# Dummy matmuls of a GAT and gated-GNN kernel: a float32 product with 64 columns in place of a bfloat16 product with 256

## The chip, the cores and the metric

The kernel runs on one core of one Trainium2 chip. The metric is the device time of one execution in microseconds (us). A core has five engines that run side by side: TensorE (PE in the profile, with its weight loads as PEld), VectorE (DVE), ScalarE (ACT), GpSimd (POOL) and SyncE (SP), which issues most of the transfers.

## The reference

A batch of 32 graphs with 512 nodes and 128 features goes through two layers that share one adjacency matrix. Cut to what is computed:

```python
# layer 0: graph attention, with a residual
h = relu(layernorm(x)) @ W                       # (32, 512, 128)
logits = leaky_relu(h @ a_src [:, :, None] + h @ a_dst [:, None, :], 0.2)
alpha = softmax(logits + where(adj > 0, 0, -1e9))
x = x + leaky_relu(alpha @ h + b, 0.3)
# layer 1: five steps of a gated recurrence, with a residual
h = relu(layernorm(x))
for _ in range(5):
    m = adj @ h                                  # used for in and out matrix alike
    z = sigmoid([m, m] @ w3.T + b3 + h @ u3.T + bu3)
    r = sigmoid([m, m] @ w4.T + b4 + h @ u3.T + bu3)
    hv = tanh([m, m] @ w5.T + b5 + (r * h) @ u5.T + bu5)
    h = (1 - z) * h + z * hv
x = x + h
```

## The kernel before, in words

Each of the 32 graphs is one tile of work: 512 nodes as four blocks of 128. Layer 0 of a graph normalizes `x` on VectorE and ScalarE, transposes it (`t_a`, L707, for the first four graphs; by transfers for the others), multiplies by the attention weights (`hp`, L812), spreads the source scores over the partitions (`es`, L847, again for the first four), weighs the adjacency (`pt`, L897) and averages (`av`, L928). Each of the five steps of layer 1 multiplies by the adjacency in two float16 halves (`m`, L1037), makes the gates (`g`, L1056, L1057 and L1077) and the candidate (`v`, L1100 and L1101), and updates the state `hT` on VectorE. The last graph has an ending of its own, with `v_end` (L1288) and `end` (L1276 and L1306).

Ahead of the graphs, TensorE turns the weight matrix (`gwT_ps`, L456), multiplies it by the attention vectors (`wa_ps`, L463: a float32 product with two columns), and turns the adjacency (`at_ps`, L494) once its 1 MB has arrived in `a_sb`.

The order of the instructions on each engine is not found while the kernel runs. Every piece of work is a `Task` with an engine, an estimated length, a key and the tasks that it needs. `plan` simulates the engines with the constants in `COST` and gives the tasks back in the order of their simulated begins; they are issued in that order, and `pin` keeps it. An engine then works through its list strictly in that order and waits at an instruction whose inputs are not there.

The change touches one kind of task, the dummy matmul. There are `FIRST_IDLE` = 32 and `IDLE` = 36 of them, 68 in all. Nothing needs them and nothing reads what they write, which is one tile of PSUM, the bank `f_idle`. Their key is 1e12, so the planner takes one for TensorE where no other task can begin, the first 32 from 500 ns of its own time on and the rest from 6500 ns on. Their estimated lengths are these:

```python
    for i in range(FIRST_IDLE + IDLE):
        add("PE", [480 if i < FIRST_IDLE else 256], 1e12, idle, (), (f_idle,),
            at=500 if i < FIRST_IDLE else 6500)
```

Both operands are views of a constant 1.0 that the start of the program writes with GpSimd.

Of the kernel before, what the change touches and what calls it, by code (L numbers as in the profile page):

```python
# [10 lines left out]
F32 = mybir.dt.float32  # L11
# [4 lines left out]
P = 128  # L16
# [272 lines left out]
def gat_then_gated_gnn_kernel(  # L289
# [20 lines left out]
    nc = tc.nc  # L310
# [23 lines left out]
    def new(buffer, name, shape=(P, N), dtype=F32):  # L334
        tag = buffer.tags[0]
        if "bank" in buffer.tags:
            buffer.tile = psum.tile([P, N], F32, tag="bank", name=name)
        elif tag in ("way", "turn", "line"):
            buffer.tile = dram.tile(list(shape), F32, tag=tag, name=name)
        else:  # L340
            buffer.tile = pools[BUFFERS[tag]].tile(list(shape), dtype, tag=tag, name=name)
        return buffer.tile
# [94 lines left out]


    f_idle = Buffer("v", "bank")
    unit = nc.const_aps.tensor(1.0, [P, 2 * P], mybir.dt.bfloat16)  # L440

    def idle():
        pin(nc.tensor.matmul(  # L443
            (f_idle.tile or new(f_idle, "idle"))[:, : 2 * P], lhsT=unit[:, :P], rhs=unit,
            start=True, stop=True,
        ))

# [3 lines that stand above are left out]
# [946 lines left out]
```

## Time and profile before

| | before |
|---|---|
| median of 3 runs | 1136.21 us (1136.18 to 1140.1) |
| profiled execution, its own time | 1136.34 us |
| profiled execution, its span | 1134.6 us |
| PE busy | 1127.7 us, 99% of the span |
| DVE busy | 875.4 us, 77% |
| ACT busy | 661.5 us, 58% |
| POOL busy | 351.5 us, 31% |
| dummy matmuls (L443) | 68 instructions, 11.5 us busy |

The span runs from the first to the last instruction; the execution's own time has 1.7 us more. A busy PE is not a PE at its peak: matmuls are pipelined, and the profile gives each a modelled end, so that their records overlap. How long a matmul occupies the engine is therefore read from the distance of one start to the next, not from its duration. One product in the program can be several records: a float32 product shows as two matmuls and two weight loads, a bfloat16 or float16 product as one of each.

### The profile page before, as it was taken

The page shows a single profiled execution, that of the slowest core. Times are in us where ns is not written, and L with a number is a line of the kernel's source. Part 1 is how long each engine was busy: PE and PEld are TensorE (multiplying, and loading weights), DVE is VectorE, ACT ScalarE, POOL GpSimd, SP SyncE. Part 2 cuts the span into 40 slices and gives each one's busy share as a digit, 9 for nine tenths or more (in the row PEclk, how much of TensorE's full clock was granted, in tenths as well). Part 3 has the DMA queues.
Part 4 walks back from the last instruction along what each step waited for, and adds up shares of the span by engine and source line. Part 5 has one row for each costly group of instructions (what it writes and reads, how often), then busy time and mean ns, then how long its engine had stood idle before and what let it go on. Part 6 is the DMA issues. An engine that isn't in the chain of part 4 may idle for free.

```text
span 1134.6 us, 14335 instructions
## 1 busy us (share of the span) xinstructions
PE 1127.7 (99%) x4334; PEld 592.6 (52%) x4334; DVE 875.4 (77%) x2002; ACT 661.5 (58%) x1299; POOL 351.5 (31%) x504
## 2 busy tenths in 40 slices
PE   9999999999999999999999999999999999999998
PEld 8655555455455545555544555555555554444444
DVE  7888968887687788879777777889888976745655
ACT  6756656645655565656566556665656564555553
POOL 4255432511431344244134214453544230100000
PEclk9999999999999999999999999999999999999999
DMA  3245453643444554355345345454655343331321
GB/s 108 57 88 112 84 108 84 126 88 84 105 81 102 85 121 93 86 120 106 89 102 107 73 100 103 111 101 114 117 116 103 75 76 84 47 74 29 84 74 67
DMA packets 188498, 104.52 MB, mean 92 GB/s; under 512 B 152192, under 2 KB 167680, under 8 KB 188288
## 3 DMA queue, kind: packets, MB, share of 16 engines
q1 hardware_dynamic: 170512, 66.57, 25.4%
q0 software_dynamic: 17472, 36.79, 17.6%
q8 instruction: 36, 0.59, 0.2%
q14 instruction: 46, 0.38, 0.1%
q10 hardware_dynamic: 432, 0.20, 0.1%
HBM read 39.46 MB, written 30.47 MB: 62 GB/s over the span
## 4 chain that ended last, share of the span: by engine, by line
PE 99%; DMA 0%; DVE 0%; SPq 0%; issue 0%; DVEq 0%
PE m L1037 24%; PE g L1077 12%; PE g L1057 12%; PE g L1056 12%; PE v L1101 12%; PE v L1100 12%; PE av L928 10%; PE hp L812 3%; DMA a_sb<-in_adj_dram 0%; PE idle L443 0%; PE at_ps L494 0%; PE t_b L707 0%; PE t_a L707 0%; PE es L847 0%; PE v_end L1288 0%; PE end L1306 0%
## 5 line engine op out<-in xcount | busy, mean ns | idle before, releaser
L1062 ACT ACTIVATE rs<-g,zrb 128x512 f32<-128x512 f32 x160 | 109.6, 685 | 122.7 <-PE g L1057 121.9
L1114 DVE SCALAR_TENSOR_TENSOR d<-hv,hT 128x512 f32<-128x512 f32 x158 | 108.2, 685 | 92.9 <-ACT hv L1107 91.9
L1107 ACT ACTIVATE hv<-v,vb 128x512 f32<-128x512 f32 x159 | 108.8, 684 | 106.6 <-PE v L1101 106.3
L1069 DVE SCALAR_TENSOR_TENSOR rh<-rs,hT 128x512 f32<-128x512 f32 x160 | 109.5, 685 | 71.2 <-ACT rs L1062 70.5
L1056 PE MATMUL g<-hT,u3T 128*128 128x512 f32 x320 | 163.4, 592 | 0.0
L1057 PE MATMUL g<-mT,w4sT 128*128 128x512 f32 x320 | 163.4, 592 | 0.0
L1077 PE MATMUL g<-mT,w3dT 128*128 128x512 f32 x320 | 162.8, 593 | 0.0
L1101 PE MATMUL v<-rh,u5hT 128*128 128x512 f32 x318 | 162.4, 592 | 0.0
L1100 PE MATMUL v<-mT,w5sT 128*128 128x512 f32 x318 | 162.4, 592 | 0.0
L1037 PE MATMUL m<-adjT,hi 128*128 128x512 f16 x640 | 161.9, 379 | 0.0
L1037 PE MATMUL m<-adjT,lo 128*128 128x512 f16 x640 | 160.7, 379 | 0.0
L650 POOL TENSOR_TENSOR rs_b<-ve_b,mhalf 128x4 f32<-128x4 f32 x32 | 36.9, 1154 | 384.2 <-DVE ve_b L630 161.4
L1089 ACT ACTIVATE zs<-g,zrb 128x512 f32<-128x512 f32 x160 | 109.4, 685 | 68.0 <-PE g L1077 66.7
L1048 ACT COPY mT<-m 128x512 f32<-128x512 f32 x160 | 92.9, 583 | 81.7 <-PE m L1037 79.1
L928 PEld LDWEIGHTS av<-hw,pt 128*128 128x128 f32 x1024 | 123.5, 191 | 21.1 <-issue 17.5
L928 PE MATMUL av<-hw,pt 128*128 128x129 f32 x1024 | 125.0, 275 | 0.1
L1123 DVE SCALAR_TENSOR_TENSOR hT<-d,hT 128x512 f32<-128x512 f32 x158 | 109.3, 692 | 11.9
L1237 ACT CAST hiT<-hT 128x512 f16<-128x512 f32 x128 | 78.9, 616 | 66.2 <-DVE hT L1123 64.2
L1037 PEld LDWEIGHTS <-hi 128*128 128x128 f16 x640 | 62.6, 98 | 98.6 <-issue 45.0
L1120 DVE SCALAR_TENSOR_TENSOR d<-zs,d 128x512 f32<-128x512 f32 x158 | 109.2, 691 | 5.2
L1037 PEld LDWEIGHTS <-lo 128*128 128x128 f16 x640 | 62.6, 98 | 90.5 <-issue 25.3
L1240 DVE TENSOR_TENSOR loT<-hT,hiT 128x512 f16<-128x512 f32 x128 | 87.6, 687 | 17.7 <-ACT hiT L1237 16.3
(141 smaller groups left out, 1351.7 us busy)
## 6 DMA issues: line engine op xcount, KB each, us to landing
x<-in_x_dram SPq DMA_DIRECT2D x32, 256.0 KB, 2.9
out_dram<-res SPq DMA_DIRECT2D x31, 256.0 KB, 2.3
turn_a<-blocks_a POOLq DMA_DIRECT2D x112, 64.0 KB, 2.7
h0T<-turn_a POOLq DMA_DIRECT2D x28, 256.0 KB, 4.0
es<-line POOLq DMA_DIRECT2D x28, 256.0 KB, 4.3
turn_b<-blocks_b POOLq DMA_DIRECT2D x112, 64.0 KB, 2.6
hT<-turn_b POOLq DMA_DIRECT2D x28, 256.0 KB, 3.9
way<-blocks SPq DMA_DIRECT2D x28, 256.0 KB, 2.3
```

Source lines behind the costliest of these rows:

```text
L928: pin(nc.tensor.matmul(avs()[:, i, :], lhsT=f_pts[c].tile[:, ts(2 * part + i, P)], rhs=hw()[:, c, : D + 1], start=start, stop=(c == K - 1) ...
L1037: pin(nc.tensor.matmul(f_m.tile, lhsT=part[:, k, :], rhs=adjT[:, k, :], start=(first and k == 0), stop=(not first and k == K - 1),))
L1056: pin(nc.tensor.matmul(g, lhsT=u3T, rhs=hT, start=True, stop=False))
L1057: pin(nc.tensor.matmul(g, lhsT=w4sT, rhs=f_mT.tile, start=False, stop=True))
L1062: pin(nc.scalar.activation(new(f_r, f"rs_{b}_{step}"), f_g.tile, AF.Tanh, bias=rb, scale=0.5))
L1069: pin(nc.vector.scalar_tensor_tensor(new(f_rh, f"rh_{b}_{step}"), f_r.tile, 1.0, hT, ALU.add, ALU.mult))
L1077: pin(nc.tensor.matmul(f_g.tile, lhsT=w3dT, rhs=f_mT.tile, start=False, stop=True, skip_group_check=True))
L1089: pin(nc.scalar.activation(new(f_z, f"zs_{b}_{step}"), f_g.tile, AF.Tanh, bias=zb, scale=0.5))
L1100: pin(nc.tensor.matmul(v, lhsT=w5sT, rhs=f_mT.tile, start=True, stop=False))
L1101: pin(nc.tensor.matmul(v, lhsT=u5hT, rhs=f_rh.tile, start=False, stop=True))
L1120: pin(nc.vector.scalar_tensor_tensor(d, f_z.tile, 1.0, d, ALU.add, ALU.mult))
L1123: pin(nc.vector.scalar_tensor_tensor(hT, f_d.tile, 0.5, hT, ALU.mult, ALU.add))
```

## The change

The constant becomes a float32 matrix of 128 x 128 in place of a bfloat16 one of 128 x 256. The dummy product takes the whole of it as the stationary operand and its first 64 columns as the moving one, and writes 64 columns of the PSUM tile in place of 256. The number of dummy tasks, their keys and their estimated lengths stay, so the planner's order stays too.

```diff
     f_idle = Buffer("v", "bank")
-    unit = nc.const_aps.tensor(1.0, [P, 2 * P], mybir.dt.bfloat16)
+    unit = nc.const_aps.tensor(1.0, [P, P], F32)
 
     def idle():
         pin(nc.tensor.matmul(
-            (f_idle.tile or new(f_idle, "idle"))[:, : 2 * P], lhsT=unit[:, :P], rhs=unit,
+            (f_idle.tile or new(f_idle, "idle"))[:, : P // 2], lhsT=unit, rhs=unit[:, : P // 2],
             start=True, stop=True,
         ))
```

## The prediction

> **What bounds the kernel now.** I read the page's busy times and its chain first, to learn whether PE time is worth anything, then PE's waits, then PE's timeline around the dummy matmuls. The page:
>
> ```profile
> PE 1127.7 (99%) x4334; PEld 592.6 (52%) x4334; DVE 875.4 (77%) x2002; ACT 661.5 (58%) x1299; POOL 351.5 (31%) x504
> PE 99%; DMA 0%; DVE 0%; SPq 0%; issue 0%; DVEq 0%
> ```
>
> The chain that ended last is PE for 99% of the span. All that PE ever waited for is in its list of waits over the whole run:
>
> ```profile
> PE at_ps L494 <- DMA a_sb<-in_adj_dram: 1.1, 1, 1.1
> PE idle L443 <- PEq L1384: 0.8, 1, 0.8
> PE end L1306 <- DVE gated L1299: 0.2, 1, 0.2
> ```
>
> Two lie in the first 8 us and one at the end. In the 1100 us between, PE goes from one product to the next, so a nanosecond added to PE there moves the end by a nanosecond, whatever the other engines do. This list can miss waits of up to 0.16 us, because a record's modelled end lies that far beyond the 0.11 us after which the next may start; so I look for cover in the distances of starts. The dummies are at these places of PE's timeline up to 8 us:
>
> ```profile
> 0.78 3.45 PE L443 MATMUL idle<-const-bfloat16-1.0 128*128 128x256 bf16 x17 [0.78 <-PEq L1384]
> 4.07 0.27 PE L456 MATMUL gwT_ps<-ident,gw 128*128 128x128 f32 x1
> 4.18 0.61 PE L443 MATMUL idle<-const-bfloat16-1.0 128*128 128x256 bf16 x4
> 4.70 0.38 PE L463 MATMUL wa_ps<-acols,gwT 128*128 128x2 f32 x2
> 4.94 1.16 PE L443 MATMUL idle<-const-bfloat16-1.0 128*128 128x256 bf16 x9
> ```
>
> The reader is to see 30 dummies in a prologue that ends with the wait for the adjacency, at 7.22 us. The other 38 stand in groups of one to seven: 28 from 8.7 to 31 us, then one at 106, 978 and 990 us and seven at 1014.5 us. Of these two windows are typical:
>
> ```profile
> 17.82 0.94 PE L443 MATMUL idle<-const-bfloat16-1.0 128*128 128x256 bf16 x7
> 18.60 0.28 PE L812 MATMUL hp<-wrow,h0T 128*128 128x131 f32 x1
> ...
> 1014.45 0.94 PE L443 MATMUL idle<-const-bfloat16-1.0 128*128 128x256 bf16 x7
> 1015.23 1.03 PE L1037 MATMUL m<-adjT,hi 128*128 128x512 f16 x4
> ```
>
> Seven dummies take 0.78 us from their first start to that of the next product in both: 0.111 us each, and the next product follows without a gap. The dummies fill what the planner took for a gap; in the trace the gap is not longer than they are.
>
> In the first block the starts lie about 0.215 us apart up to 3.72 us (0.94, 1.16, 1.37 and so on), and 0.11 us from there. PE ran at half pace for 2.94 us after its first matmul, although the page shows the granted clock as full.
>
> [...]
> - [...] `v` at L1100 with 512 columns starts at 31.06 and the next product at 31.93, 0.87 us, against 0.217 us for a float16 product with 512 columns (four of `m` in 0.87 us): a factor of 4.0. So 4 x 64 columns stream as long as 1 x 256.
> - [...] 190 ns for a float32 load (`viol_ps`), 99 ns for a bfloat16 one (`idle`).
> [...]
>
> **The change part by part.** It removes 68 bfloat16 products, one load and one matmul each, and adds 68 float32 products, two of each. The order, the bank, the other engines' lists and all transfers stay, and no wait is added: nothing waits for a dummy. The float32 constant is no new work either, since GpSimd writes const-float32-1.0 in the program's start already, at 0.29 us. What remains is one question: **how long does PE need for a float32 product with 64 columns?** The trace has none. Its bounds:
> - Below: the streaming alone, 4 x 64 columns at the pace of the 512-column product, 0.87 / 8 = 0.109 us. That equals the old 0.111; a gain is excluded, because the columns have to stream.
> - Above: two loads that both show, 2 x 0.11 = 0.22 us. Dense `av` records, one load each, start every 0.111 us with a float32 load in each, so a load can't take longer than that in a stream.
> - Nearest row: float32 products with two columns, where nothing streams. For `viol_ps` (PE and PEld in turn):
>
> ```profile
> 938.30 0.28 PE L588 MATMUL viol_ps<-viol,ones 128*128 128x2 f32 x2
> 938.44 1.02 PE L1037 MATMUL m<-adjT,hi 128*128 128x512 f16 x4
> ...
> 938.09 0.41 PEld L588 LDWEIGHTS viol_ps<-viol,ones 128*128 128x128 f32 x2
> 938.33 0.64 PEld L1037 LDWEIGHTS <-hi 128*128 128x128 f16 x4
> ```
>
> Its two matmuls start at 938.30 and 938.33, the next load at 938.33, and the next product at 938.44: 0.14 us for the pair, 0.03 from pass to pass and 0.11 for the load of the product behind. `wa_ps` shows the same: its second load at 4.80, the next load at 4.83, the next product at 4.94. With 64 columns the first pass streams 0.109 / 2 = 0.054 us in place of 0.03, and the second, also 0.054, lies beneath the 0.11 of the next load. I take 0.054 + 0.11 = **0.163 us**, 0.052 more than before, and at half pace double, 0.326 against 0.215.
>
> Prologue (30 dummies), with the same moment of full pace, 3.72 us: 2.94 / 0.326 = 9 dummies go by until then, the other 8 take 1.30, so `gwT_ps` starts at 5.02 in place of 4.07: +0.95. From there to `wa_ps` the four dummies take 0.11 + 4 x 0.163 = 0.76 against 0.62 (where PE waited for ScalarE's copy `gwT`): +0.14. Nine more: +0.47. Together 1.56 us. The cover is the wait for the adjacency: the last dummy starts at about 5.83, `at_ps` could start at 5.94 and starts at 7.22, so 1.28 us are hidden; without that transfer all 1.56 would show. **+0.28** is left. Behind the later `wa_ps` stand ScalarE's four small copies to `wrow` (5.12 to 5.5, then about 6.5), which `hp` needs at 8.95: hidden by 2 us. VectorE's normalization of the first graph needs no PE.
>
> The other 38: 38 x 0.052 = **+1.98**. Cover: two dummies start at 11.42 and 11.53, and `av` could start at 11.64 but starts at 11.86, 0.22 us; `g` at 29.77 is 0.06 late. What these wait for comes from PE itself a little before and moves along, so I count about half, **-0.15**. Everywhere else the next product starts at once, and nothing hides the addition. After 31 us the whole train is late by the same amount.
>
> Sum: 0.28 + 1.98 - 0.15 = +2.1 us. The profiled execution's own time is 1136.34, which becomes 1138.4; it lies 0.13 above the median of 1136.21, so I predict **1138.3** for the median. The 0.163 has both ends: at 0.109, nothing changes (1136.2). At 0.22 (0.43 at half pace) the prologue gains 1.89 + 0.37 + 0.98 - 1.28 = 1.96, the others 38 x 0.11 - 0.15 = 4.03, +6.0 together: 1142.2.
>
> **The rivals.**
> - *The loads hide* (no change, 1136.2). For it: in a dense stream of `av` each float32 load lies beneath 129 columns at no visible cost. Against: beneath 64 columns there is half the time, and `viol_ps` shows 0.11 for the load behind it.
> - *Both loads show* (1142.2). For it: `wa_ps` has its two loads 0.11 apart, and 190 ns records. Against: the 0.03 from pass to pass.
> - *PE stays at half pace* (slower). [...] a float32 dummy streams only 0.109 of 0.163 us, two thirds of its time. If that isn't enough, the 30 dummies go at 0.326 us, `at_ps` starts at about 0.78 + 30 x 0.326 + 0.2 = 10.8 in place of 7.22 (+3.5), real products then run at half pace for up to another 2.94 us (+1.5), and the other 38 add 2.0: +7.0, **1143.2**. It decides if the pace has not changed when the 30 dummies are through. [...]
> - *The change doesn't do what it says*: the planner's lengths would have to move the order, but they are constants; I give it nothing.
>
> **How the numbers follow.** The forecast gets 0.62, the hidden loads 0.18, both loads 0.12, half pace 0.06, a cost above my bounds 0.02. A difference of 0.5%, 5.7 us, is about what a measurement of this kernel can tell from no change (one of three runs lay 0.35% off). The forecast and the hidden loads fall within it, but for 0.02 of the latter below; both loads lie on its edge, half each; half pace is 0.05 outside. That makes 0.02 faster, 0.85 the same, 0.13 slower. The range takes in the hidden loads with a little scatter, 1135.8, and reaches to both loads, 1142.5.
>
> **What would show it right or wrong.** Right: 136 matmul records at L443, pairs 0.16 us apart, seven of them in 1.14 us at 17.8 us; full pace at about 3.7 us; the wait for the adjacency down to zero, `at_ps` at 7.5; from 32 us on all products 1.6 us later, the end 2.1 later. Wrong: pairs at 0.11 or 0.22 us, a half pace that goes on to `at_ps`, or new waits of PE after 32 us.

## The result and the profile after

The changed kernel is slower: 1148.12 us median of 6 runs (1147.47 to 1148.78), against 1140.01 for the kernel before (1136.18 to 1141.07) measured beside it. The ratio is 1.0088, with a 95% interval of 1.0073 to 1.0103. The profiled executions have 1147.68 and 1136.34 us, spans of 1145.9 and 1134.6, so 11.3 us more. The medians lie closer together because the times of the kernel before stand in groups, near 1136.3 and from 1138 to 1141, and four of the six here are late ones. In the larger samples beside the experiments its median is 1136.62 us (35 runs) and 1137.75 (38), so that the 8.1 us between the medians here understate the loss. The last experiment looks at where the groups come from.

The page of the changed kernel, its busy times and its chain:

```profile
PE 1140.2 (100%) x4402; PEld 608.2 (53%) x4402; DVE 876.2 (76%) x2002; ACT 662.2 (58%) x1299; POOL 351.4 (31%) x504
PE 99%; DVE 0%; issue 0%; DVEq 0%
```

PE has 68 records more, 12.5 us more busy time, and still is the chain. All its waits over the run:

```profile
PE idle L443 <- PEq L1384: 0.8, 1, 0.8
PE end L1306 <- DVE gated L1299: 0.2, 1, 0.2
```

The wait for the adjacency, 1.1 us before, is gone: the 1 MB is there, and PE comes to it late. PE's timeline (start, length, line, tile, count) up to the turning of the adjacency and a little beyond:

```profile
0.78 7.49 PE L443 MATMUL idle<-const-float32-1.0 128*128 128x64 f32 x34 [0.78 <-PEq L1384]
8.06 0.42 PE L456 MATMUL gwT_ps<-ident,gw 128*128 128x128 f32 x1
8.27 1.81 PE L443 MATMUL idle<-const-float32-1.0 128*128 128x64 f32 x8
9.87 0.53 PE L463 MATMUL wa_ps<-acols,gwT 128*128 128x2 f32 x2
10.27 4.08 PE L443 MATMUL idle<-const-float32-1.0 128*128 128x64 f32 x18
14.14 1.06 PE L494 MATMUL at_ps<-ident,a_sb 128*128 128x128 f32 x4
14.99 1.06 PE L707 MATMUL t_a<-ident,h 128*128 128x128 f32 x4
15.85 1.01 PE L494 MATMUL at_ps<-ident,a_sb 128*128 128x128 f32 x4
16.69 0.56 PE L443 MATMUL idle<-const-float32-1.0 128*128 128x64 f32 x4
17.09 1.11 PE L812 MATMUL hp<-wrow,h0T 128*128 128x131 f32 x8
```

The first 34 records take 7.28 us up to `gwT_ps`, 0.214 each and **0.43 us a dummy**, and the pace does not change: PE runs at half pace up to 14.14 us. The real products from there still take 0.21 us each (four of `t_a` from 14.99 to 15.85); only at about 16.6 us are they through at 0.11 and less. Two later windows show a dummy at full pace:

```profile
26.45 1.67 PE L443 MATMUL idle<-const-float32-1.0 128*128 128x64 f32 x14
27.96 0.67 PE L812 MATMUL hp<-wrow,h0T 128*128 128x131 f32 x4
...
1025.07 1.67 PE L443 MATMUL idle<-const-float32-1.0 128*128 128x64 f32 x14
1026.58 1.89 PE L1037 MATMUL m<-adjT,hi 128*128 128x512 f16 x8
```

Fourteen records, seven dummies, take 1.51 us from their first start to that of the next product: **0.216 us a dummy** in both, against 0.111 before and 0.163 in the forecast. Within the series the starts lie 0.112 us apart (the second record starts at 26.51, the fourteenth at 27.85). Only the first step is shorter, 0.056.

The starts of the same products in the two profiles give the account. The lines of the kernel before on which its second row rests:

```profile
8.72 0.38 PE L443 MATMUL idle<-const-bfloat16-1.0 128*128 128x256 bf16 x2
8.95 1.13 PE L812 MATMUL hp<-wrow,h0T 128*128 128x131 f32 x8
```

| product | before | after | late by |
|---|---|---|---|
| first `at_ps` | 7.22 | 14.14 | 6.92 |
| first `hp` | 8.95 | 17.09 | 8.14 |
| `hp` behind seven dummies | 18.60 | 27.96 | 9.36 |
| first `v` (L1100) | 31.06 | 41.51 | 10.45 |
| `m` behind the last seven | 1015.23 | 1026.58 | 11.35 |

So 6.9 us are lost in the prologue. Between `at_ps` and `hp` 1.2 are lost, of which the two dummies there make 0.17 (0.40 against 0.23) and the real products at half pace the other 1.05. The 36 dummies behind add 3.2. At 0.105 us more for each, all 38 would add 4.0 where 3.4 show; about 0.6 fell into gaps that were there. One such gap is the 0.22 us ahead of `av`: from the first of the two dummies to `av` it is 0.44 us before (11.42 to 11.86) and 0.43 after (19.61 to 20.04).

### The profile page after: what moved, and what is told of

It reads as the page before. It is cut to its first block, busy times and chain, and to the rows that moved or that the text cites. A ratio compares the mean times of both kernels' runs of the same rounds, so it can differ in the third digit from the quotient of the medians.

```text
span 1145.9 us, 14471 instructions
## 1 busy us (share of the span) xinstructions
PE 1140.2 (100%) x4402; PEld 608.2 (53%) x4402; DVE 876.2 (76%) x2002; ACT 662.2 (58%) x1299; POOL 351.4 (31%) x504
## 4 chain that ended last, share of the span: by engine, by line
PE 99%; DVE 0%; issue 0%; DVEq 0%
PE m L1037 24%; PE g L1077 12%; PE g L1056 12%; PE g L1057 12%; PE v L1100 12%; PE v L1101 12%; PE av L928 10%; PE hp L812 3%; PE idle L443 2%; PE at_ps L494 0%; PE t_a L707 0%; PE es L847 0%; PE t_b L707 0%; PE v_end L1288 0%; PE end L1306 0%; PE end L1276 0%
## 5 line engine op out<-in xcount | busy, mean ns | idle before, releaser
L1100 PE MATMUL v<-mT,w5sT 128*128 128x512 f32 x318 | 162.4, 592 | 0.0
L1057 PEld LDWEIGHTS g<-mT,w4sT 128*128 128x128 f32 x320 | 60.8, 190 | 76.5 <-issue 69.8
```

What stands on the lines that cost most here:

```text
L1057: pin(nc.tensor.matmul(g, lhsT=w4sT, rhs=f_mT.tile, start=False, stop=True))
L1100: pin(nc.tensor.matmul(v, lhsT=w5sT, rhs=f_mT.tile, start=True, stop=False))
```

## The experiments

The theory has two parts. First, a pass of a float32 product (one of its two matmul records) has a length that its columns do not set: 0.112 us within a series and 0.213 at half pace. So 64 columns would cost what 128 do. I took the load of the weights for the cause, a supposition from the load records (median 192 ns for these dummies, 99 ns for the bfloat16 ones before). Second, columns then stream only about half of the time (by estimate 0.054 us of a pass, half of the 0.109 that 4 x 64 columns take at the pace of the 512-column product), and with that PE does not come to full pace. The rivals: full pace came late by chance; float32 dummies do not bring it at all; or the loss lies elsewhere.

### Only half as many dummies

```diff
-        add("PE", [480 if i < FIRST_IDLE else 256], 1e12, idle, (), (f_idle,),
+        add("PE", [480 if i < FIRST_IDLE else 256], 1e12, idle if i % 2 else lambda: None, (), (f_idle,),
```

> Every second dummy is left out, so 34 float32 products with 64 columns stand where 68 did; a float32 pair takes 0.215 us at full pace and a bfloat16 product 0.11, so PE's time for dummies is that of the kernel before. Theory (the dummies keep PE occupied but do not bring it to full pace): about 15 of them at 0.43 us end near 7.3 us, the adjacency is turned from there at half pace, and the first 12 products of it add about 1.3 us; the time is about 1137.8. Rival (occupancy alone, full pace came late by chance): full pace near 3.7 us, adjacency at 7.2, 1136.3.

Measured: 1138.41 us median (1137.57 to 1140.97), ratio 1.0005 (0.9990 to 1.0019). PE's timeline in its profile, whose own time is 1140.82:

```profile
0.78 3.65 PE L443 MATMUL idle<-const-float32-1.0 128*128 128x64 f32 x16 [0.78 <-PEq L1384]
5.57 2.37 PE L443 MATMUL idle<-const-float32-1.0 128*128 128x64 f32 x10
9.47 1.13 PE L494 MATMUL at_ps<-ident,a_sb 128*128 128x128 f32 x4 [1.52 <-DMA a_sb<-in_adj_dram]
10.40 1.06 PE L707 MATMUL t_a<-ident,h 128*128 128x128 f32 x4
12.42 1.81 PE L812 MATMUL hp<-wrow,h0T 128*128 128x131 f32 x8
```

The real products run at half pace (0.21 each in `t_a`) into those of `hp`: the dummies again did not bring full pace. In this execution the adjacency came at 9.47 us in place of 7.2, which the last experiment takes up; eight of the twelve runs lie from 1137.57 to 1138.81, near the expected 1137.8. Most of the loss goes with half of the PE time. That leaves the question why the pace stayed.

### The same length, more columns streaming

```diff
-            (f_idle.tile or new(f_idle, "idle"))[:, : P // 2], lhsT=unit, rhs=unit[:, : P // 2],
+            (f_idle.tile or new(f_idle, "idle"))[:, :P], lhsT=unit, rhs=unit,
```

> The dummies are float32 with 128 columns[...]. At full pace they should occupy PE as long as those with 64 columns, 0.215 us. Theory of the share ([...]): full pace near 3.7 us, the adjacency turned near 9.2 us, time about 1136.3 + 2 + 4 = 1142.3. Rival of the type (float32 dummies do not count as activity): half pace beyond 14 us as in the changed kernel, 1147.7.

Measured: 1142.36 us (1141.86 to 1143.78), ratio 1.0045 (1.0032 to 1.0058).

```profile
0.78 5.61 PE L443 MATMUL idle<-const-float32-1.0 128*128 128x128 f32 x34 [0.78 <-PEq L1384]
6.23 0.27 PE L456 MATMUL gwT_ps<-ident,gw 128*128 128x128 f32 x1
7.38 2.25 PE L443 MATMUL idle<-const-float32-1.0 128*128 128x128 f32 x18
9.47 0.64 PE L494 MATMUL at_ps<-ident,a_sb 128*128 128x128 f32 x4
15.23 1.05 PE L443 MATMUL idle<-const-float32-1.0 128*128 128x128 f32 x8
16.12 2.84 PE L928 MATMUL av<-hw,pt 128*128 128x129 f32 x24
```

Twice the columns make the kernel 5.8 us shorter than the changed one. The last eight records take 0.89 us, 0.112 from start to start, so a dummy is as long as with 64 columns. But the first 34 take only 5.45 us: their starts lie 0.213 apart up to 3.90 us and 0.112 from 4.11 on, so the pace changed at about 4.1 us. Full pace came with float32 dummies, and the rival of the type falls. Here little but the length is left: `at_ps` is 2.25 us late, and of the 6.92 in the changed kernel the other 4.7 go with the half pace.

### Prologue and the rest, apart

```diff
+        if i >= FIRST_IDLE:     # in the second run: i < FIRST_IDLE; the lines around are left out
+            pin(nc.tensor.matmul(t[:, : P // 2], lhsT=unit32, rhs=unit32[:, : P // 2], start=True, stop=True))
+        else:
+            pin(nc.tensor.matmul(t[:, : 2 * P], lhsT=unit[:, :P], rhs=unit, start=True, stop=True))
```

With bfloat16 in the prologue:

> The first 32 dummies, which fill the prologue, are bfloat16 with 256 columns as before, the other 36 float32 with 64. Theory ([...]): the adjacency is turned near 7.2 us at full pace, and the 36 add 36 x 0.105 = 3.8 us less about 0.2 of gaps: 1139.9. Rival (0.163 us a pair, as predicted, and the rest of the loss is all in the prologue): 36 x 0.052 = 1.9, 1138.1.

With float32 in the prologue:

> The first 32 dummies are float32 with 64 columns, the other 36 bfloat16 with 256 as before. Theory: half pace through the prologue, the adjacency turned near 14.1 us, 6.9 later than before, its products at half pace for another 1.2 us, and nothing after: about 1136.3 + 8.1 = 1144.3. Rival (half the loss is later, with the 36): 1141.

Measured: 1139.85 us (1139.38 to 1144.0), ratio 1.0032 (1.0020 to 1.0044), with bfloat16 in the prologue; 1144.22 us (1144.18 to 1145.35), ratio 1.0057 (1.0033 to 1.0080), with float32 there. Against 1136.3, the lower group of the kernel before, that is 3.5 and 7.9, together 11.4. The two parts add up to the whole loss, 11.3 between the profiled executions, so nothing is lost elsewhere.

### Where enough columns stream

```diff
-            ... [:, : P // 2], lhsT=unit, rhs=unit[:, : P // 2],
+            ... [:, : 3 * P // 4], lhsT=unit, rhs=unit[:, : 3 * P // 4],     # then 80, then 2
```

Ninety-six columns:

> The dummies are float32 with 96 columns: [...] three quarters, between the half at which full pace did not come and the whole at which it came. All other things are those of the changed kernel. Theory of the share: if three quarters are enough, the adjacency is turned near 9.4 us and the time is that of 128 columns, 1142.3; if not, near 14.1 us and 1147.7. A rival in which the clock counts the columns that went by since the start would bring full pace after 2 x 13.7 x 128 / 96 passes at most, inside the prologue, and a time between, near 1143.

Eighty:

> The dummies are float32 with 80 columns: [...] five eighths, between the half at which full pace did not come and the three quarters at which it came. The length of a pair should be 0.215 us as before. If five eighths are enough: full pace near 4 us, the adjacency turned near 9.5 us, 1142.6. If not: 14.1 us and 1147.7. A result between would mean that the date of full pace depends on the share and not only whether it comes.

Two:

> The dummies are float32 with 2 columns, like wa_ps and viol_ps, so almost nothing streams. Theory ([...]): pairs at 0.215 us at full pace and 0.43 at half, half pace through the prologue, the adjacency turned near 14.1 us, 1147.7 as with 64 columns. Rival (the reading of the prediction, 0.03 from pass to pass and 0.11 for the load behind, so 0.14 a pair): 0.28 us at half pace, the adjacency turned near 9.5 us, about 1136.3 + 2.3 + 1.2 + 38 x 0.03 = 1141.

| columns | share of a pass that streams (estimate) | `at_ps` | median |
|---|---|---|---|
| 2 | almost none | 14.10 | 1148.35 (1147.99 to 1148.88) |
| 64 | 1/2 | 14.14 | 1148.12 (1147.47 to 1148.78) |
| 80 | 5/8 | 14.19 | 1148.72 (1147.32 to 1149.09) |
| 96 | 3/4 | 9.57 | 1142.77 (1142.49 to 1144.41) |
| 128 | 1 | 9.47 | 1142.36 (1141.86 to 1143.78) |

The time has two levels and steps between 80 and 96 columns. The rival of counted columns, which asked for a time near 1143 from a late change of pace and is near it by coincidence at 96, falls with 80: at 96 columns the pace changed at about 4.45 us, after 17 records, and at 80 all 60 records of the prologue go by without a change, in which three times as many columns stream. The first 34 records at 80 and at 96 columns, one line of each timeline:

```profile
0.78 7.51 PE L443 MATMUL idle<-const-float32-1.0 128*128 128x80 f32 x34 [0.78 <-PEq L1384]
```

```profile
0.78 5.75 PE L443 MATMUL idle<-const-float32-1.0 128*128 128x96 f32 x34 [0.78 <-PEq L1384]
```

The shares are estimates: the 0.109 us of 4 x 64 columns make 0.054 us a pass for 64 columns, 0.068 for 80, 0.082 for 96 and 0.109 for 128, out of the 0.112 from start to start, in round fractions.

Chance is no rival for this step, though the date of full pace does vary. With dummies that by the same estimate stream all the time it is 3.7 us in the kernel before, 3.5 and 4.4 in its two profiles of the last experiment, about 4.1 with four bfloat16 products a dummy, and 5.8 and 6.1 in two profiles with bfloat16 in the prologue (`gwT_ps` starts at 4.36 and takes 0.21 in both). With 2, 64 and 80 columns it had not come at 14.1 us in any of four profiles, and none of the 14 runs with these columns throughout lies below 1147.3 us; none of the 22 with 96 and 128 lies above 1144.5.

The run with two columns is for the length. Its seven dummies late in the kernel:

```profile
1025.88 1.62 PE L443 MATMUL idle<-const-float32-1.0 128*128 128x2 f32 x14
1027.36 1.89 PE L1037 MATMUL m<-adjT,hi 128*128 128x512 f16 x8
```

That is 1.48 us for fourteen passes in which, by estimate (2/128 of 0.109 us), almost nothing streams. The first step is 0.028 us, and the other thirteen are 0.112 each, as with 64, 80, 96 and 128 columns; at half pace they are 0.213. So the length of a pass does not come from its columns. I read the steps as loads: the first beneath the product ahead, the other thirteen in view, and a short one for the float16 product behind. For this speak the load records (median 192 ns in this run) and the short bfloat16 products of the next experiment. That it is the load, and not another fixed cost of a float32 pass, was not shown; no run changed the number of weights.

### As many columns with more loads

```diff
-        pin(nc.tensor.matmul(
-            (f_idle.tile or new(f_idle, "idle"))[:, : 2 * P], lhsT=unit[:, :P], rhs=unit, ...
+        for _ in range(4):
+            pin(nc.tensor.matmul(
+                (f_idle.tile or new(f_idle, "idle"))[:, : P // 2], lhsT=unit[:, :P], rhs=unit[:, : P // 2], ...
```

> Each dummy is four bfloat16 products with 64 columns, so 256 columns as before, with four loads in place of one. Theory (a bfloat16 load is short, about 0.03 us as behind viol_ps, and the loss is that of the float32 load): four take 4 x 0.03 = 0.12 us at full pace, columns stream nearly all the time, full pace comes near 4 us, and the time is within 1 us of 1136.3. Rival ([...]): 0.43 us a dummy, half pace through the prologue, 1156 or more. Between them, 0.055 a product: 0.22 us a dummy and half the time streaming, which by the share theory gives the changed kernel's 1147.7.

Measured: 1140.41 us (1136.86 to 1142.82), ratio 1.0013 (0.9998 to 1.0028).

```profile
4.42 0.68 PE L444 MATMUL idle<-const-bfloat16-1.0 128*128 128x64 bf16 x16
4.94 0.38 PE L464 MATMUL wa_ps<-acols,gwT 128*128 128x2 f32 x2
9.22 0.75 PE L495 MATMUL at_ps<-ident,a_sb 128*128 128x128 f32 x4 [2.73 <-DMA a_sb<-in_adj_dram]
```

Sixteen products take 0.52 us, 0.033 each and 0.13 a dummy, not the rival's 0.43: a bfloat16 product with 128 weights and 64 columns takes less than a third of the 0.112 us of a float32 pass. In the prologue the products lie 0.053 us apart up to 4.11 us and 0.033 from 4.15 on, so full pace came as expected, with four times as many products. The median is 4 us off the expectation; the profile, taken near it at 1140.31, shows the adjacency at 9.22 us and a new wait of 0.9 us at `av`, so the time says little here and the pace much.

### Fewer dummies or none

```diff
-        add("PE", [480 if i < FIRST_IDLE else 256], 1e12, idle, (), (f_idle,),
+        add("PE", [480 if i < FIRST_IDLE else 256], 1e12, idle if i < FIRST_IDLE else lambda: None, (), (f_idle,),
```

> Bfloat16 with 256 columns as in the kernel before, but only the first 32 dummies; the 36 behind the prologue are left out, the order of all else stays. Theory (the later dummies stand where PE has no real wait, so they cost their whole length): 36 x 0.11 = 4.0 us less, with 0.3 given back by waits that now show: 1132.6. Rival (they fill waits that are there without them): PE waits in their place, and the time is 1136.3.

And with no dummy at all, where every one of these tasks issues nothing:

> No dummy at all, all else as in the kernel before. Theory: the adjacency is turned near 7.2 us at half pace, the first 3 us of real products take 1.5 us longer, and the 36 later ones are saved as in the run with the first 32 alone: 1132.6 + 1.5 = 1134.1, so less than the kernel before. Rival (without dummies PE's short waits in the first 30 us keep it at half pace far longer, since PE then streams too little): 1140 or more.

Measured: 1135.57 us (1135.17 to 1140.48), ratio 0.9985 (0.9969 to 1.0000), with the first 32 alone; 1138.15 us (1136.79 to 1139.75), ratio 0.9997 (0.9986 to 1.0009), with none. Both expectations missed, by 3 and by 4 us. PE's waits with the first 32 alone, where the kernel before has none between 8 us and the end:

```profile
PE av L928 <- DVE pt L897: 1.0, 3, 0.6
PE g L1077 <- ACT rs L1062: 0.3, 1, 0.3
PE m L1037 <- DMA hi<-hiT: 0.2, 1, 0.2
```

The later dummies stand where PE would wait, for most of their length: leaving out 4 us of them shows 1.5 us of waits that the list sees and saves 0.7 us against 1136.3. The interval of the ratio reaches 1.0000, so it does not tell this kernel from the one before. But the eight runs of its lower group (1135.17 to 1135.66) all lie below the shortest run of the kernel before (1135.97). With no dummy the adjacency is turned from 7.13 us at half pace, and full pace comes at about 10.5 us. Between the two medians lie 2.6 us, and between the profiled executions (1137.1 and 1135.6) the 1.5 expected; the base was set too low for both. So the dummies of the prologue are worth something here, and the 36 behind it cost a little or nothing.

### The groups of the kernel before

> The kernel before, unchanged, for another profile. Its times stand in two groups, near 1136.3 and near 1140.2. Theory: in the later group the adjacency lands late, near 9.3 us in place of 7.2, as the profiles with half the dummies and with bfloat16 at 64 columns show; then a profile whose own time is near 1140 has at_ps near 9.3 us, and one near 1136.3 has it near 7.2. Rival: the groups differ in the moment of full pace, and the landing is the same in both.

> The kernel before once more, for the same question: a profile near 1140 with the adjacency turned near 9.3 us, or near 1136.3 with 7.2 us, by the theory; by the rival the landing is the same in both and the moment of full pace differs.

The two profiles have 1140.18 and 1138.86 us. The first:

```profile
9.52 0.75 PE L494 MATMUL at_ps<-ident,a_sb 128*128 128x128 f32 x4 [3.43 <-DMA a_sb<-in_adj_dram]
10.75 1.06 PE L494 MATMUL at_ps<-ident,a_sb 128*128 128x128 f32 x4
12.03 1.90 PE L812 MATMUL hp<-wrow,h0T 128*128 128x131 f32 x8
```

and the second:

```profile
9.64 0.75 PE L494 MATMUL at_ps<-ident,a_sb 128*128 128x128 f32 x4 [3.23 <-DMA a_sb<-in_adj_dram]
10.67 0.65 PE L494 MATMUL at_ps<-ident,a_sb 128*128 128x128 f32 x4
11.38 1.13 PE L812 MATMUL hp<-wrow,h0T 128*128 128x131 f32 x8
```

Both have the adjacency 2.3 to 2.4 us late. The first also fell to half pace, 0.8 us after its wait of 3.43 us had ended (four of `at_ps` in 0.85 us, eight of `hp` in 1.73); the second, after 3.23, did not (0.48 and 0.96). So the theory and its rival each hold half: the landing makes 1136.3 into 1138.9, and a lapse of the pace makes it 1140.2. The mean granted clock over the run is 0.998 in the first profile and 0.999 in the second; 3.4 us at half pace, from about 10.3 to 13.8 us by the starts, would by estimate take 0.0015 off it. So the lapse can be looked for in the mean granted clock of every run. Of the 80 runs of the kernel before beside the experiments, 28 took 1139.67 us or more, and 27 of these have 0.996 to 0.998; of the other 52, 51 have 0.999 or 1.000. Whether the length of the wait, 3.43 us with a lapse and 3.23 without, has to do with it was not tried. The changed kernel, which comes to the adjacency at 14 us, has neither, and its times lie within 1.3 us. Why the transfer lands at two dates was not tried.

## Why the prediction was wrong

- **That PE's time is the metric** held. No new wait came, the wait for the adjacency went to zero, and the loss goes through to the end (6.9, then 8.1, then 11.35 us). This is so for time added: of the 4.0 us of dummies taken away in one experiment only 0.7 came back.
- **The length of a dummy** failed: 0.216 us at full pace, not 0.163, so the 38 later ones added 3.4 (0.17 and 3.2), not 1.98; the cover was about 0.6, not 0.15. The step is the reading of `viol_ps`. I took the 0.03 us between its two matmul records for the change from pass to pass, and the 0.11 behind it for the float16 load of the next product. The run with two columns has 0.028 once and then 0.112 thirteen times, so the short step is the one at the edge and 0.112 is the one of the series; the pair's 0.14 was the length of the edge. A matmul's recorded start did not tell that its load had ended: the second `viol_ps` record starts 0.03 us after its load record does, and that record is 0.19 long. The upper bound, 0.22, was the value. Its reason, two loads that both show, stays a supposition, to which 190 ns against 99 in the load records had pointed.
- **The moment of full pace** failed, and with it the prologue: +6.9 us in place of +0.28, and another 1.05 on real products that the sum put at nothing. The sum took 3.72 us from the old profile as if it belonged to the chip. It changed with the columns of the dummies (about 4.45 us with 96, after 14.1 us with 80), and even with the old dummies it lay between 3.5 and 6.1 us. The half pace was a rival with 0.06, worked with the wrong length.
- **The rivals were taken one at a time.** The length at the upper bound and the half pace came together: 0.112 us a pass at full pace, 0.213 at half, and half pace beyond 14 us. With 0.43 a dummy the rival's own sum gives 0.78 + 30 x 0.43 + 0.2 = 13.9 for `at_ps`, near the 14.14 measured. Of its half pace for real products, 1.5 us, 1.05 came.
- **The range** ended at 1142.5, where the longer pass without the lasting half pace lies: 128 columns, which have just that, measured 1142.36.
- **A busy PE was not yet at full pace.** PE was busy by its records from 0.78 us on in the changed kernel, and full pace took until about 16.6 us, when real products had come. With dummies that by estimate stream all the time it took 2.7 to 5.3 us from the first matmul.

What stays open is why full pace came with some dummies and not with others. With 80 float32 columns it had not come after 13 us of dummies, with 96 it came at about 4.45 us; that the share of time in which columns stream decides is an explanation of mine, and the runs did not tell it apart from something that goes with the columns. That the load makes the length of a float32 pass was not shown either.

## What to carry to other kernels

Equal numbers of column passes are not equal times. A float32 product here was two passes of 0.112 us, whether 2 or 128 columns streamed, where a bfloat16 product of 64 columns took 0.033 from start to start; so a matmul with few columns is to be priced by its passes, from the starts within a long series. Where matmuls are there to bring PE to full pace, the date has to be read from the starts: here it came with 96 and 128 float32 columns (about 4.45 and 4.1 us) and with bfloat16 products of 64 and 256 columns (about 4.1 and 3.5 to 6.1 us), and not by 14.1 us with 2, 64 and 80 float32 columns. And where two unknowns of a forecast feed on each other, their joint case needs a sum of its own.

## What the runs showed of the hardware that was not expected

- A float32 pass takes 0.112 us from start to start with 2, 64, 80, 96 and 128 columns, and near twice that at half pace. With two columns, where by estimate almost nothing streams, it is 0.213 there. The prediction doubled its length at half pace without a run that showed it; the run with two columns does.
- The step from 80 to 96 columns moves the time by 5.9 us (1148.72 and 1142.77), and none of the five widths gave a time between.
- The date of full pace differs by up to 2.6 us between executions with bfloat16 dummies in the prologue (3.5 to 6.1 us).
- PE's recorded clock is 1.00 in every stretch of the first 20 us, both in the profile of the kernel before and in that of the changed one, while the starts show half pace up to 3.72 us and to about 16.6 us. The profile with the later lapse has a mean of 0.998. So the pace of the first stretch was read from the distances of starts.
